# Two pairs' places 960 to 1008 sorted in one pass, and the next pair's first rows gathered beside a node sort

## The chip, the cores and the metric

The kernel runs on one core of one Trainium2 chip. The metric is device time in microseconds (us) for one execution. Before the change the median of three executions was 3306.28 us (3271.85 to 3311.16).

## What is computed

There are 16 graphs of 1024 nodes, each node with 64 channels. Layer 0 is the part that the change touches. It normalises and clips the nodes, drops some edges of nodes with many neighbours, and then takes for every node and channel three quantiles over the node's remaining neighbours:

```python
vals = jnp.where(nd[..., None], x[:, None, :, :], jnp.inf)
s = jnp.sort(vals, axis=2)
nv = nd.sum(2)
for tau, w in zip((0.25, 0.5, 0.75), (0.25, 0.5, 0.25)):
    pos = tau * jnp.maximum(nv - 1, 0)
    lo, hi = jnp.floor(pos), jnp.ceil(pos)
    agg = agg + w * (v_lo + (pos - lo) * (v_hi - v_lo))
```

The sum goes through two small matmuls and is added to x. Layer 1 is three graph convolutions with the whole adjacency and a last matmul.

## The kernel before

**Places.** The graphs are handled as 8 pairs, p = 0 to 7, with the two graphs of a pair in the upper and lower 64 partitions. The nodes of a graph are ordered by their number of neighbours, and a node's position in that order is its place. Places with similar counts share a sorting network with a fixed number of slots. Places 0 to 640 are three *blocks* (0: 200 places with 11 slots, 1: 192 with 13, 2: 248 with 15), places 640 to 960 are three groups of *nodes* (17, 19 and 21 slots), 960 to 1008 are one more block, called MID here (48 places, 26 slots), and 1008 to 1024 are the TAIL (16 places, 42 slots).

**How rows get to their slots.** For a block, `gather` (L1115) makes one-hot matrices `s` on VectorE (L1143) for two or more slots at a time, and TensorE multiplies them with the node values `hp` into PSUM (L1174); ScalarE copies the result to the tile `g` (L1179). The values are in three bfloat16 parts, `st.hp`, and no such matmul can run before the third part is written (L698). There are two buffers for `s`. For nodes, GpSimd issues one indirect DMA for each slot and graph (`ask`, L1287), 34, 38 or 42 for a sort; here they are called asks. Their target `gn` is one buffer, so a new set of asks starts when the sort before it has read its rows.

**How rows are sorted.** `quantiles` (L1070) runs a network of min and max on VectorE (L1081), each instruction over several slots at once, multiplies the ranks that are wanted with coefficients (L1093) and adds them up (L1102). An instruction's width is the number of compared slots times the places. TAIL is sorted for four pairs at once: a pair's TAIL rows go to DRAM (`tail_d`, L1230), and `rows_of_pairs` (L1251) loads them beside each other. MID is sorted for each pair alone.

**The order.** For each of the pairs 0 to 6 the loop runs these stages one after the other; `weave` (L1335) puts steps of other work between the instructions of a sort, at set shares of it:

1. sort block 0, with the gather of block 1 and asks;
2. sort nodes, with the gather of block 2;
3. sort block 1, with asks for the next nodes;
4. sort block 2, with the gathers of MID and TAIL and asks;
5. sort nodes, with the last 9 steps (`steps(4)`) of `prepare` for pair p+1;
6. after pair 4 only: sort the TAIL of pairs 0 to 3;
7. sort MID of pair p, with the gather of block 0 of pair p+1 and 0.4 of the asks for the next nodes.

Through all of it the steps of `prepare(p + 1)` (L637) are spread: loading the adjacency, dropping edges, listing the rows, numbering the slots, writing `hp`. Pair 7 has the same stages after the loop, with `later` woven in instead: the two dense layers of all pairs. `later` begins by fetching the sums of a pair with 16 indirect DMAs (L1474), and VectorE adds them up (L1371).

The order in the source is not the order on the engines: a planner in the framework estimates when each instruction is ready and sorts each engine's stream by it. Every engine then runs its own stream strictly in order, so that an instruction which waits holds up all that stand behind it on its engine.

**Tags.** Tiles with one tag share a buffer: `g0` holds the rows of blocks 0 and 2 and the TAIL rows of several pairs, `g1` those of block 1 and MID.

Of the kernel before, what the change touches and what calls it, by code (L numbers as in the profile page):

```python
# [406 lines left out]
def graph_layers_kernel(ctx: ExitStack, tc: tile.TileContext, ins, out: bass.AP):  # L407
# [187 lines left out]
    def layernorm_relu(pool, h, xt, sq, T):  # L595
# [17 lines left out]
    live_d = [dram.tile([N, N // 4], I32, name=f"live_d{b}") for b in range(NB)]  # L613
    MW, TW = (b[1] - b[0] for b in (BLOCKS[MID], TAIL))
    part_d = {
        MID + 1: [dram.tile([P, TAIL[3], TW], F32, name=f"tail_d{p}") for p in range(NP)],
    }

    with tc.tile_pool(name="setup_fill", bufs=1) as setup:
# [5 lines left out]
                nc.scalar.dma_start(out=rows_d[p][x * ROWS + ZERO_ROW : x * ROWS + BIG_ROW + 1, :], in_=filler)  # L625

    part_z = {
        MID: const.tile([P, len(TAUS), 1, MW], BF16, name="mid_z"),
        MID + 1: const.tile([P, len(TAUS), NP, TW], BF16, name="tail_z"),
    }  # L630
    place = const.tile([P, NB, NT], I32, name="place")
# [478 lines left out]
    def per_group(block):  # L1110

        W = block[1] - block[0]
        return max(1, min(HALF // W, 400 // W))
# [98 lines left out]
    def gather_block(st, n, pools, home=None, into=None, first=-0.2, end=0.9):  # L1212


        work, ps, rows = pools
        block = (BLOCKS + (TAIL,))[n]
        j0, j1, _, slots = block
        pool, tag, bufs = home or (rows, f"g{n % 2}", 1)

        def groups():  # L1220
            if n >= MID:
                z = part_z[n]
                nc.scalar.copy(z[:, :, st.p % z.shape[2], :], st.z[:, :, slice(*held(block))])
            to = into
            if to is None:
                to = st.g[n] = pool.tile([P, slots, j1 - j0], F32, tag=tag, bufs=bufs, name="g")
            send(pools, (yield from gather(st, block, to, pools)))
            in_place = n == MID or st.p == NP - 1
            if n >= MID and not in_place:
                nc.scalar.dma_start(out=part_d[n][st.p][:, :, :], in_=to)  # L1230

        return Steps(groups()), -(-slots // per_group(block)), first, end

    def sort_block(st, n, pools):

        work, ps, rows = pools
        block = BLOCKS[n]
        j0, j1, _, slots = block
        if n == 0:

            send(pools, st.gathered)
            st.agg = work.tile([P, SPLIT], F32, tag="agg", bufs=1, name="agg")
            st.done = 0
        t = rows.tile([P, plan(block)[3], j1 - j0], F32, tag="t", bufs=1, name="t")
        yield from quantiles(work, block, (st.g[n], t), st.z[:, :, j0:j1], st.agg[:, j0:j1])
        while st.done + P <= j1:
            cols = slice(st.done, st.done + P)
            waiting.append((st.p, st.agg, cols, st.done))
            st.done = cols.stop

    def rows_of_pairs(n, first, end, sent, pools, tag):  # L1251

        work, ps, rows = pools
        block = (BLOCKS + (TAIL,))[n]
        W = block[1] - block[0]
        g = rows.tile([P, block[3], (end - first) * W], F32, tag=tag, bufs=1, name="g_pairs")
        for p in range(first, sent):
            nc.scalar.dma_start(out=g[:, :, (p - first) * W : (p - first + 1) * W], in_=part_d[n][p][:, :, :])
        return g
# [42 lines left out]
    def asking(fetched, first, end, share=1.0):  # L1302

        return fetched[4], math.ceil(share * NODES[fetched[1]][3]), first, end
# [346 lines left out]
    with ExitStack() as stack:  # L1651
        keep = stack.enter_context(tc.tile_pool(name="keep", bufs=1))
        pools = (
            stack.enter_context(tc.tile_pool(name="work", bufs=1)),
            stack.enter_context(tc.tile_pool(name="ps", bufs=1, space=PSUM)),
            stack.enter_context(tc.tile_pool(name="rows", bufs=1)),
        )
        with ExitStack() as inner:
            early = (
                inner.enter_context(tc.tile_pool(name="early", bufs=1)), keep,  # L1660
                inner.enter_context(tc.tile_pool(name="ps_early", bufs=1, space=PSUM)),
            )
            ahead = Steps(prepare(0, early))
            ahead.rest()
            sts = [ahead.result]
            jobs = iter(NODE_ORDER)

            def fetch_next(tag="gn"):
                pairs, i = next(jobs)
                return fetch_nodes([sts[p] for p in pairs], i, pools, tag)  # L1670

            nodes = fetch_next()
            nodes[4].rest()
            first, *_ = gather_block(sts[0], 0, pools)
            first.rest()
            for p in range(NP - 1):
                st = sts[p]
                ahead = Steps(prepare(p + 1, early))

                def steps(n):  # L1680
                    return ahead, SHARES[n], 0.0, 1.0

                weave(sort_block(st, 0, pools), gather_block(st, 1, pools), asking(nodes, 0.0, 0.9), steps(0))
                weave(sort_nodes(nodes, pools), gather_block(st, 2, pools), steps(1))
                nodes = fetch_next()
                weave(sort_block(st, 1, pools), asking(nodes, 0.1, 1.0, 0.4), steps(2))
                send_nodes()
                both = rows_of_pairs(MID, p, p + 1, p, pools, "g1")
                weave(
                    sort_block(st, 2, pools), gather_block(st, MID, pools, into=both),  # L1690
                    gather_block(st, MID + 1, pools, (early[0], "a", 2)), asking(nodes, 0.0, 0.7), steps(3),
                )
                if p in TAILS:
                    tails = rows_of_pairs(MID + 1, *TAILS[p], TAILS[p][1], pools, "g0")
                weave(sort_nodes(nodes, pools), steps(4))
                ahead.rest()
                sts.append(ahead.result)
                nodes = fetch_next()
                if p in TAILS:
                    weave(sort_pairs(MID + 1, *TAILS[p], tails, pools))  # L1700
                    send(pools)
                weave(
                    sort_pairs(MID, p, p + 1, both, pools), gather_block(sts[-1], 0, pools, first=0.3, end=1.0),
                    asking(nodes, 0.0, 1.0, 0.4),
                )


        with ExitStack() as inner:
            one = inner.enter_context(tc.tile_pool(name="late", bufs=1))
            late = (one, inner.enter_context(tc.tile_pool(name="ps_late", bufs=2, space=PSUM)))  # L1710
            done = Pair()
            done.sent = 4
            ahead = Steps(later(late, keep, done))
            def steps(n):
                return ahead, LATE_SHARES[n], 0.0, 1.0

            st = sts[-1]
            weave(sort_block(st, 0, pools), gather_block(st, 1, pools), asking(nodes, 0.0, 0.9), steps(0))
            weave(sort_nodes(nodes, pools), gather_block(st, 2, pools), steps(1))
            nodes = fetch_next()  # L1720
            then = [fetch_next("r0")]
            weave(sort_block(st, 1, pools), asking(nodes, 0.0, 0.9), steps(2))
            send_nodes()
            both = rows_of_pairs(MID, NP - 1, NP, NP - 1, pools, "g1")
            weave(
                sort_block(st, 2, pools), gather_block(st, MID, pools, into=both), asking(then[0], 0.0, 0.9), steps(3)
            )
            tails = rows_of_pairs(MID + 1, *TAILS[NP - 1], NP - 1, pools, "g0")
            weave(sort_nodes(nodes, pools), gather_block(st, MID + 1, pools, into=tails[:, :, -TW:]), steps(4))
            then += [fetch_next(), fetch_next("s"), fetch_next("s")]  # L1730
            weave(
                sort_pairs(MID + 1, *TAILS[NP - 1], tails, pools), asking(then[1], 0.0, 0.5), asking(then[2], 0.5, 1.0),
                steps(5),
            )
            send(pools)
            done.sent = NP - 2
            weave(sort_nodes(then[0], pools), asking(then[3], 0.0, 1.0), steps(6))
            send_nodes()
            weave(sort_pairs(MID, NP - 1, NP, both, pools), steps(7))
            send(pools)  # L1740
            weave(sort_nodes(then[1], pools), steps(8))
            send_nodes()
            done.sent = NP - 1
            weave(sort_nodes(then[2], pools), steps(9))
            send_nodes()
            weave(sort_nodes(then[3], pools), steps(10))
            send(pools)
            done.sent = NP
            ahead.rest()
# [46 lines left out]
```

## Time and profile before

| | us |
|---|---|
| median of three executions | 3306.28 |
| the profiled execution | 3037.03 |
| its span, first to last instruction | 3035.3 |
| VectorE busy (L1081 is its largest line) | 2410.4 |
| TensorE busy, mean granted clock 0.861 | 2116.4 |
| GpSimd busy, most of it L1287 | 1551.3 |
| the 744 asks L1287 | 1182.9 |
| pair 0: nodes (second), MID, then block 0 of pair 1 | 42.8 + 39.2 + 43.2 |
| pair 4: nodes, TAIL, MID, then block 0 of pair 5 | 44.4 + 60.8 + 33.0 + 46.4 |
| pair 6: nodes, MID, then block 0 of pair 7 | 49.4 + 91.0 + 39.1 |
| last MID sort, of pair 7 | 55.8 |

The profiled execution took 269 us less than the median. The rows by stage run from one sort's last addition on VectorE to the next one's. Loop and preparation take the first 2208 us; the rest is pair 7 and the dense layers.

### The profile page before, as it was taken

How to read it: one execution, taken by the hardware profiler on the slowest of the kernel's cores; microseconds unless marked ns; L12 is line 12 of the kernel's file. 1: busy time of each engine (PE TensorE's matmuls, PEld its weight loads, DVE VectorE, ACT ScalarE, POOL GpSimd, SP SyncE). 2: the span in 40 equal slices, each digit the busy share in tenths (PEclk: the TensorE clock that was granted, in tenths of full speed). 3: DMA queues.
4: the chain of work that ended last, by engine and by line, in shares of the span. 5: the costliest groups of instructions: out<-in, count | busy, mean ns of one | idle time of the engine just before them, and what ended most of it. 6: DMA issues, size and time to landing. Idle time of an engine off the chain costs nothing. (4 is left out here: it accounts for less than half of the span.)

```text
span 3035.3 us, 58595 instructions
## 1 busy us (share of the span) xinstructions
PE 2116.4 (70%) x23385; PEld 1480.7 (49%) x23401; DVE 2410.4 (79%) x5602; ACT 1563.8 (52%) x3060; POOL 1551.3 (51%) x1155
## 2 busy tenths in 40 slices
PE   1748876886887688678627886886368487067768
PEld 0435744663565466356414753663256264034446
DVE  3238989999998999999899999998378489268732
ACT  2775775676487468557634775687023123022212
POOL 5115556385645738564675285374834768730110
PEclk9879988997998899799858997997689698588889
DMA  4214123322321332232312221412211242112211
GB/s 120 73 45 124 56 68 73 102 65 62 99 91 46 75 99 62 62 109 86 65 36 67 88 63 51 135 56 52 67 19 21 64 85 69 25 21 53 56 50 44
DMA packets 261051, 205.54 MB, mean 68 GB/s; under 512 B 217120, under 2 KB 217248, under 8 KB 256672
## 3 DMA queue, kind: packets, MB, share of 16 engines
q1 hardware_dynamic: 165120, 131.39, 15.1%
q0 software_dynamic: 39680, 62.23, 8.3%
q10 hardware_dynamic: 55968, 8.09, 1.6%
q8 instruction: 185, 3.03, 0.4%
q14 instruction: 98, 0.80, 0.1%
HBM read 148.82 MB, written 52.75 MB: 66 GB/s over the span
## 5 line engine op out<-in xcount | busy, mean ns | idle before, releaser
L1287 POOL DMA_INDIRECT g_nodes<-rows_d,rows_listed x744 | 1182.9, 1590 | 907.0 <-DVE prod L1093 310.5
L1174 PE MATMUL pg<-s,hp 128*64 128x248 bf16 (+6 forms) x12048 | 888.1, 301 | 171.7 <-DVE s L1143 150.2
L1174 PEld LDWEIGHTS <-hp 128*64 128x64 bf16 x12048 | 656.8, 114 | 349.3 <-DVE s L1143 101.5
L1143 DVE TENSOR_SCALAR s<-r 128x3200 bf16<-128x3200 bf16 (+19 forms) x856 | 406.1, 523 | 36.0 <-PE pg L1174 34.8
L1429 PE MATMUL pg<-adjT,xw 128*64 128x512 fp8e4 x2304 | 282.3, 399 | 60.2 <-ACT xw L1418 56.3
L1474 POOL DMA_INDIRECT agg<-agg_d,place x128 | 131.4, 1027 | 275.3 <-DVE rest L1417 138.5
L890 POOL DMA_INDIRECT live_d<-edge,place x128 | 170.7, 1334 | 146.5 <-DVE place L883 108.4
L1429 PEld LDWEIGHTS <-xw 128*64 128x64 bf16 x2304 | 149.2, 115 | 177.4 <-ACT xw L1418 64.2
L787 PE MATMUL ptE<-ident_h,edge 128*128 128x128 bf16 x1024 | 86.1, 236 | 212.6 <-ACT edge L780 191.7
L1179 ACT COPY g<-pg 128x248 f32<-128x248 f32 (+3 forms) x238 | 97.7, 411 | 247.3 <-PE pg L1174 246.7
L1371 DVE TENSOR_TENSOR agg<-agg,h_late 128x1024 f32<-128x1024 f32 x8 | 9.8, 1230 | 243.1 <-DMA agg<-agg_d,place 243.1
L780 ACT ACTIVATE edge<-a 128x1024 fp8e4<-128x1024 f32 x128 | 134.7, 1054 | 95.5 <-DMA a<-in_adj 79.3
L787 PEld LDWEIGHTS <-edge 128*128 128x128 fp8e4 x1024 | 66.4, 105 | 236.6 <-ACT edge L780 199.8
L782 DVE SCALAR_TENSOR_TENSOR junk_v<-a 128x1024 fp8e4<-128x1024 f32 x128 | 155.8, 1217 | 27.7 <-DMA a<-in_adj 27.0
L1081 DVE TENSOR_TENSOR t<-g 128x800 f32<-128x800 f32 (+9 forms) x184 | 167.5, 924 | 0.9
L880 ACT ACTIVATE stays<-keys,minus 128x1024 fp8e4<-128x1024 f32 x128 | 143.3, 1119 | 37.5 <-PE keys L872 32.7
L1081 DVE TENSOR_TENSOR g<-t 128x992 f32<-128x992 f32 (+7 forms) x176 | 160.0, 932 | 1.8
L924 PE MATMUL pt<-ident_h,lp 128*128 128x128 bf16 x1024 | 94.3, 250 | 89.5 <-DMA lp<-live_d 43.2
L834 ACT ACTIVATE stays<-cs,back 128x1024 f16<-128x1024 f32 x128 | 137.1, 1113 | 34.2 <-DVE look L815 16.0
L861 ACT ACTIVATE edge<-q,bias 128x1024 fp8e4<-128x1024 f32 x128 | 141.8, 1109 | 17.4 <-PE q L856 16.7
L1081 DVE TENSOR_TENSOR t_nodes<-g_nodes 128x256 f32<-128x256 f32 (+6 forms) x192 | 125.2, 659 | 31.8 <-DMA g_nodes<-rows_d,rows_listed 19.2
L790 ACT ACTIVATE edgeT<-ptE 128x1024 fp8e4<-128x1024 f32 x128 | 129.8, 1038 | 17.3 <-PE ptE L787 16.5
(241 smaller groups left out, 4530.8 us busy)
## 6 DMA issues: line engine op xcount, KB each, us to landing
a<-in_adj SPq DMA_DIRECT2D x128, 512.0 KB
adjT_d<-edgeT SPq DMA_DIRECT2D x16, 1024.0 KB
lp<-live_d POOLq DMA_DIRECT2D x32, 512.0 KB
adjT<-adjT_d SPq DMA_DIRECT2D x16, 1024.0 KB
g_nodes<-rows_d,rows_listed POOLq DMA_INDIRECT x744
room<-in_x SPq DMA_DIRECT2D x16, 256.0 KB
h_d<-room SPq DMA_DIRECT2D x16, 256.0 KB
rows_d<-room SPq DMA_DIRECT2D x64, 64.0 KB
```

Of the source, the lines that this page charges most:

```text
L780: nc.scalar.activation(edge[:, t, :], a, AF.Sign, saturate=False)
L782: nc.vector.scalar_tensor_tensor(junk, a, 1.0, a, ALU.is_equal, ALU.not_equal, accum_out=odd[:, b, t : t + 1], saturate=False)
L787: nc.tensor.matmul(out=pt[:, u, :], lhsT=edge[:, t, u * P : (u + 1) * P], rhs=ident_h, start=True, stop=True)
L834: nc.scalar.activation(stays[:, t, :], cs, AF.Abs, bias=back[:, t : t + 1], scale=2.0)
L861: nc.scalar.activation(edge[:, t, :], q, AF.Relu, bias=bias(-2.0), accum_out=nv[:, t : t + 1], saturate=False)
L880: nc.scalar.activation(junk, keys, AF.Sign, bias=minus[:, t : t + 1], accum_out=above[:, t : t + 1], saturate=False)
L890: sent = nc.gpsimd.indirect_dma_start(out=live_d[b][:, :], out_offset=bass.IndirectOffsetOnAxis(ap=place[:, b, t : t + 1], axis=0), in_=ed ...
L1081: nc.vector.tensor_tensor(view(bufs, o, n1, n2), view(bufs, a, n1, n2), view(bufs, b, n1, n2), ALU.max if op else ALU.min)
L1143: nc.vector.tensor_scalar(s[:, k, :, us, w0:], r[:, :, us, at + w0 : at + W], float(LIVE + 1 + k0 + k), None, ALU.is_equal)
L1174: summed = nc.tensor.matmul(out=pg[x * C : (x + 1) * C, ks, w0:], lhsT=st.hp[:, part, x, u, :], rhs=s[:, ks, x, u, w0:], start=(whole and ...
L1287: nc.gpsimd.indirect_dma_start(out=g[:, k, a * C : (a + 1) * C], out_offset=None, in_=rows_d[st.p][:, :], in_offset=bass.IndirectOffsetOnA ...
L1429: nc.tensor.matmul(out=pg[cs, :], lhsT=part[:, u, cs], rhs=adjT[x][:, u, sl], start=(u == 0 and k == 0), stop=(u == NT - 1 and k == len(xw ...
```

## The change

MID is no longer sorted after every pair, but after every odd one for that pair and the even one before it: four sorts of 96 places, where there were eight of 48. An even pair's MID rows are written to DRAM (`mid_d`) on ScalarE's queue and loaded again beside the odd pair's in stage 4 of the odd pair. With no MID sort in an even pair, the gather of block 0 of the next pair is woven with the node sort of stage 5, from half of it on, behind the last steps of `prepare`, which are squeezed into the first 0.4 of it; in pair 4 it goes with the TAIL sort. The asks that stood beside MID are given in the next stage 1 alone. The rows of several pairs' TAIL in the loop move from `g0` to `g1`. Pair 7's MID sort holds pairs 6 and 7.

```diff
@@ -613,6 +613,7 @@
     part_d = {
+        MID: [None if p % 2 else dram.tile([P, BLOCKS[MID][3], MW], F32, name=f"mid_d{p}") for p in range(NP)],
         MID + 1: [dram.tile([P, TAIL[3], TW], F32, name=f"tail_d{p}") for p in range(NP)],
     }
@@ -625,7 +626,7 @@
-        MID: const.tile([P, len(TAUS), 1, MW], BF16, name="mid_z"),
+        MID: const.tile([P, len(TAUS), 2, MW], BF16, name="mid_z"),
@@ -1225,7 +1226,7 @@
-            in_place = n == MID or st.p == NP - 1
+            in_place = (n == MID and st.p % 2) or st.p == NP - 1
             if n >= MID and not in_place:
                 nc.scalar.dma_start(out=part_d[n][st.p][:, :, :], in_=to)
@@ -1685,24 +1686,45 @@
-                both = rows_of_pairs(MID, p, p + 1, p, pools, "g1")
+                both = rows_of_pairs(MID, p - 1, p + 1, p, pools, "g1") if p % 2 else None
                 weave(
-                    sort_block(st, 2, pools), gather_block(st, MID, pools, into=both),
+                    sort_block(st, 2, pools), gather_block(st, MID, pools, into=both and both[:, :, MW:]),
                     gather_block(st, MID + 1, pools, (early[0], "a", 2)), asking(nodes, 0.0, 0.7), steps(3),
                 )
                 if p in TAILS:
-                    tails = rows_of_pairs(MID + 1, *TAILS[p], TAILS[p][1], pools, "g0")
-                weave(sort_nodes(nodes, pools), steps(4))
-                ahead.rest()
-                sts.append(ahead.result)
-                nodes = fetch_next()
-                if p in TAILS:
-                    weave(sort_pairs(MID + 1, *TAILS[p], tails, pools))
+                    tails = rows_of_pairs(MID + 1, *TAILS[p], TAILS[p][1], pools, "g1")
+
+                def coming():
+                    ahead.rest()
+                    sts.append(ahead.result)
+                    steps, *_ = gather_block(sts[-1], 0, pools)
+                    yield from steps.gen
+
+                coming = Steps(coming())
+                count = -(-BLOCKS[0][3] // per_group(BLOCKS[0]))
+                if p % 2:
+                    weave(sort_nodes(nodes, pools), steps(4))
+                    ahead.rest()
+                    coming_at = 0.3
+                elif p in TAILS:
+                    weave(sort_nodes(nodes, pools), steps(4))
+                    ahead.rest()
+                    weave(sort_pairs(MID + 1, *TAILS[p], tails, pools), (coming, count, 0.4, 1.0))
+                    coming.rest()
                     send(pools)
-                weave(
-                    sort_pairs(MID, p, p + 1, both, pools), gather_block(sts[-1], 0, pools, first=0.3, end=1.0),
-                    asking(nodes, 0.0, 1.0, 0.4),
-                )
+                else:
+                    weave(sort_nodes(nodes, pools), (ahead, SHARES[4], 0.0, 0.4), (coming, count, 0.5, 1.0))
+                    coming.rest()
+                if p % 2:
+                    coming.step()
+                    nodes = fetch_next()
+                    weave(
+                        sort_pairs(MID, p - 1, p + 1, both, pools), (coming, count, 0.3, 1.0),
+                        asking(nodes, 0.0, 1.0, 0.4),
+                    )
+                    coming.rest()
+                else:
+                    nodes = fetch_next()
@@ -1721,9 +1743,9 @@
-            both = rows_of_pairs(MID, NP - 1, NP, NP - 1, pools, "g1")
+            both = rows_of_pairs(MID, NP - 2, NP, NP - 1, pools, "g1")
             weave(
-                sort_block(st, 2, pools), gather_block(st, MID, pools, into=both), asking(then[0], 0.0, 0.9), steps(3)
+                sort_block(st, 2, pools), gather_block(st, MID, pools, into=both[:, :, MW:]), asking(then[0], 0.0, 0.9), steps(3)
             )
@@ -1736,7 +1758,7 @@
-            weave(sort_pairs(MID, NP - 1, NP, both, pools), steps(7))
+            weave(sort_pairs(MID, NP - 2, NP, both, pools), steps(7))
```

## The prediction

> **What bounds the kernel now.** I read the busy shares first, then the 40 slices, then the windows of single stages, then who waited for whom. The chain that ended last covers only the final layers and says nothing of the loop.
>
> ```profile
> PE 2116.4 (70%) x23385; PEld 1480.7 (49%) x23401; DVE 2410.4 (79%) x5602; ACT 1563.8 (52%) x3060; POOL 1551.3 (51%) x1155
> DVE  3238989999998999999899999998378489268732
> ```
>
> VectorE (DVE) is at 90% or more in the slices of the loop (260 to 2130 us), so there its instructions set the time. The next fence is the windows of pair 1: second node sort, MID, block 0 of pair 2. Columns are length, then busy us and instructions of each engine, granted clock, DMA share, GB/s.
>
> ```profile
> core 0: us, PE busy (x) PEld busy (x) DVE busy (x) ACT busy (x) POOL busy (x), PEclk, DMA share, GB/s
> 685.00:729.50 44.50, 30.76 (x264) 16.37 (x265) 41.08 (x136) 33.38 (x69) 14.02 (x13) 0.79 0.19 59
> 729.50:769.00 39.50, 26.47 (x313) 17.18 (x313) 39.16 (x120) 15.79 (x37) 35.67 (x13) 0.80 0.21 54
> 769.00:819.00 50.00, 38.74 (x456) 27.17 (x457) 44.75 (x61) 27.48 (x52) 37.25 (x25) 0.90 0.52 148
> ```
>
> MID fills VectorE (39.2 of 39.5 us) and covers 26.5 us of TensorE: the gather of the next block 0. In a timeline inside such a stage, the start of one sort instruction to the next is what it costs, less than its duration:
>
> ```profile
> 2142.32 0.35 DVE L1081 TENSOR_TENSOR t_pairs<-t_pairs 128x192 f32<-128x192 f32 x1
> 2142.59 0.25 DVE L1081 TENSOR_TENSOR t_pairs<-g_pairs 128x96 f32<-128x96 f32 x1
> 2142.76 0.35 DVE L1081 TENSOR_TENSOR t_pairs<-g_pairs,t_pairs 128x192 f32<-128x192 f32 x1
> ...
> 2148.07 0.20 DVE L1081 TENSOR_TENSOR t_pairs<-g_pairs,t_pairs 128x48 f32<-128x48 f32 x1
> 2148.19 0.38 DVE L1081 TENSOR_TENSOR g_pairs<-t_pairs,g_pairs 128x48 f32<-128x48 f32 x2
> ```
>
> Widths 192, 96 and 48 start the next after 0.27, 0.17 and 0.12 us: 1.04 ns a column and 69 ns fixed. The 0.20 to 0.35 us durations overlap, and summing them would promise twice the saving.
>
> Two waits matter: GpSimd's asks inside MID, and VectorE's wait at the end of MID of pair 6.
>
> ```profile
> 735.01 1.14 POOL L1287 DMA_INDIRECT g_nodes<-rows_d,rows_listed  x1 [0.30 <-issue]
> 736.45 11.96 POOL L1287 DMA_INDIRECT g_nodes<-rows_d,rows_listed  x1 [0.30 <-issue]
> 748.71 0.94 POOL L1287 DMA_INDIRECT g_nodes<-rows_d,rows_listed  x1 [0.30 <-issue]
> ```
>
> ```profile
> 2201.18 0.94 POOL L1474 DMA_INDIRECT agg<-agg_d,place  x1 [0.30 <-issue]
> ...
> 2203.67 1.27 DVE L1371 TENSOR_TENSOR agg<-agg,h_late 128x1024 f32<-128x1024 f32 x1 [52.22 <-DMA agg<-agg_d,place]
> ```
>
> **What the Trainium skill says.** *Vector Engine (DVE) Microarchitecture Reference*, section 5.2, gives 1.0417 ns a column and about 75 ns an instruction after overlap; the starts above agree (1.04 and 69). *SBUF — State Buffer*, section "Who interferes with whom", says that GpSimd and VectorE share a port pair that one instruction holds whole, and that a tensor_tensor with both inputs in SBUF contends with GpSimd's reads. The trace fits: an ask takes 0.94 us while VectorE is idle (2152 to 2182 us), 1.3 to 1.7 us in block 0, and two of them 10 to 15 us in a MID sort. *TensorE: Matmul & The Clock Gate*, section "What's actually happening", has the clock throttled by default and released by activity; granted clocks in my windows run from 0.60 to 0.98, low where TensorE is idle. It serves the slow rival.
>
> **The change part by part.**
>
> *Four MID sorts fewer.* A MID sort is 91 instructions (89 in pair 4) and 12,768 columns: 91 x 0.069 + 12,768 x 0.00104 = 19.6 us. Even pairs lose it: -19.6 in pairs 0 and 2, -18.9 in pair 4. An odd pair's sort keeps its 91 instructions and doubles the columns: +13.3 us each in pairs 1, 3, 5 and 7. Were nothing but VectorE in play, that is 4 x (19.6 - 13.3) = -25 us. ScalarE's stream loses 55 rows, mostly coefficients; at 52% busy I value that at nothing (cover: VectorE's sorts; without that cover, a gain under 1 us for each of four sorts).
>
> *Pairs 0 and 2: the gather loses its cover.* In the built order only four of block 0's one-hot instructions (two groups, all that two `s` buffers hold) stand inside the node sort. The third group stands behind the last write of `hp`, which stands at or after the end of the node sort. TensorE's part of this gather took 25.3 us in pair 0 (484.4 to 509.7, from 2 us after `hp`). Block 0's sort needs slots 0 to 6 first (four of six groups) and then the rest. Between `hp` and the instruction that needs the last slots, pair 0's order has seven one-hot instructions of this gather (5.7 us), four adjacency checks L782 (5.2), four one-hots of block 1 (3.3) and two 600-wide sort instructions (1.4): 15.6 us beside 25.3 + 2, so VectorE idles some 11 us, where MID hid it all. Bounds: 7 (clock 0.98 instead of 0.91) to 20 (clock 0.65). Net -8.6 in each of pairs 0 and 2.
>
> *The asks.* From the point where `gn` and its list are free to the next node sort's first instruction VectorE has some 70 us of work in these pairs, idle time included. The 34 and 38 asks at 1.7 us (block 0's pace, with gaps) need 58 and 65, plus some 2 to land. They fit, barely: 0, with 0 to +10 each. What would be late next is that node sort.
>
> *Pair 4.* The gather goes beside 60.8 us of TAIL sort, in which TensorE was busy 2.1 us. Fully covered: -18.9. The asks of that stage have TAIL and block 0, 107 us; 0. The TAIL rows in `g1` must wait for the write of `mid_d`, and ScalarE waits with them: 0 to +7, as the longest issue of such a load took 7.1 us; I take 0, because the node sort follows.
>
> *Odd pairs 1, 3, 5.* +13.3 each. The asks get that much longer, so the waits before the next node sort (5.2 us at 817, 3.5 at 1348) shrink; I take -5 in all. Sum +35.
>
> *The DRAM trip.* Writes are long rows. A load has 128 x 26 pieces of 192 bytes. ScalarE's DMA queue took 1.6% of 16 engines x 3035 us for 55,968 packets, 14 ns each, so 3328 on 16 engines are 3 us, issued a whole block 2 ahead of the sort. Its issue waits for block 1's rows in `g1`, with ScalarE's evacuations behind it: 0 to +7 for each of four; I take 0, the cover being VectorE's block 2.
>
> *Pair 6 and the dense layers.* Before, 38 asks from 2109.6 took until 2182 (two were held 11 us each by MID), then came 16 fetches of sums, and L1371 ran at 2203.7, 94 us after the start. L1371 now stands after the fourth group of the block 0 gather, and GpSimd's order has all 42 asks ahead of the fetches. VectorE reaches it 30 us after the start; 18 asks at 1.6 us, 24 at the free pace of 1.25, 16 fetches at 1.25 and the landing make 81 us. So the stall stays, about 50 us. The last two groups and the `s` buffers behind it cost 6 us more than before. Net 81 + 6 - 94 = -7, not the -19.6 of its sort. Bounds -20 and +10.
>
> *Pair 7's MID.* +13.3, but a wait of 14.4 us for L1371 (2740.7) stands in that stage, and the sort work ahead of it that runs beside the fetches costs nothing: +5, bounds 0 and 13.
>
> Sum: -17.2 - 18.9 + 35 - 7 + 5 = **-3 us** against the profiled 3037. The median of the runs is 269 us higher and the profile does not show where; I carry the difference over unscaled: 3306 - 3 = **3303 us**. This case's own range is 3268 to 3348, from the bounds above.
>
> **The rivals.**
>
> *Slower, the gather without cover (21%).* After `hp`, TensorE has block 0's 25 us, block 1's (4.6 us for each of seven groups, 32) and the next adjacency's transposes (about 10): 67 us beside some 63 of VectorE work up to the next node sort. At the clock seen there, 0.91, it just fits. If the long idle phases drop it below 0.75, the 67 become over 81 and each of pairs 0, 2 and 6 loses another 18 us or more; at 0.65, 94 and 31, so +93 - 3: 3396. For it: clocks of 0.69 and 0.65 in the windows of pair 2's node sort and pair 6's MID, and the runs' extra 269 us, which may be TensorE's. Against: in these stretches TensorE is busy almost throughout.
>
> *Faster, the stall of pair 6 goes too (15%).* If L1371's 52 us no longer block and the even gathers stay covered, it is -25 - 52 = -77: 3229. Against it stands the built order, with 58 GpSimd instructions ahead of that wait.
>
> *Nothing moves.* If the 269 us are TensorE's and it is the bound in the timed runs, both saving and cost vanish: 3306, inside the likeliest case.
>
> **Chances.** A measurement of this kernel can tell about 2% (66 us) from no change. Within it: 64%, forecast and null together. Faster by more: 15%; slower by more: 21%. The range for 8 in 10 reaches into both rivals: 3230 to 3390.
>
> **What would show it.** Right: MID sorts of 96 places near 33 us of starts; in pairs 0 and 2 idle time of 7 to 20 us on L1143 or on the first L1081 of block 0, released by TensorE; no asks of 10 us there; a 45 to 55 us wait of the first L1371. Wrong: idle over 25 us in those pairs, node sorts that wait for asks, a ScalarE held by the `mid_d` loads, or an L1371 that finds its rows.

## The result and the profile after

The changed kernel takes 3403.55 us (median of four, 3399.71 to 3406.83), the kernel before 3291.27 in the same comparison: ratio 1.034, 95% interval 1.026 to 1.042. It is 3.4% slower; forecast were 3303 us and no change. A later comparison on another chip gave 1.042 (1.031 to 1.053). All ratios here leave out executions more than 1.5% above the fastest of their kernel, so that they can differ a little from the quotient of the medians.

The page of the changed kernel, the lines that answer to those shown of before: busy time of each engine, and VectorE in the 40 slices.

```profile
PE 2235.3 (66%) x23401; PEld 1493.6 (44%) x23401; DVE 2391.6 (70%) x5238; ACT 1552.4 (46%) x2988; POOL 1331.7 (39%) x1155
DVE  4136885979879598599799975997176381388852
```

VectorE has 19 us less work than before, and yet it is at 90% or more in 11 of the 40 slices where it was in 21: it waits. The next fence is the windows of the changed kernel at three hand-overs from one pair to the next: block 0 after the node sort in pairs 0 and 2, and the sort of 96 places in pair 3. Columns are length, then busy us and instructions of each engine, TensorE's granted clock, DMA share, GB/s.

```profile
core 0: us, PE busy (x) PEld busy (x) DVE busy (x) ACT busy (x) POOL busy (x), PEclk, DMA share, GB/s
532.60:635.60 103.00, 71.78 (x740) 41.40 (x741) 62.38 (x87) 41.61 (x77) 35.04 (x34) 0.76 0.36 100
1137.50:1232.40 94.90, 64.47 (x744) 41.34 (x742) 53.43 (x80) 36.44 (x71) 37.12 (x36) 0.82 0.33 94
1406.40:1500.30 93.90, 34.82 (x374) 22.22 (x374) 57.87 (x158) 24.07 (x64) 29.22 (x31) 0.66 0.17 36
```

In each of them VectorE is idle for 36 to 41 us (length less busy time). Two waits in the first two windows make most of it, from the timeline of VectorE ("remote" is an end that the profile can put down to no instruction):

```profile
583.23 1.90 DVE L1144 TENSOR_SCALAR s<-r 128x3200 bf16<-128x3200 bf16 x2 [26.36 <-remote]
1189.61 3.37 DVE L1144 TENSOR_SCALAR s<-r 128x2688 bf16<-128x2688 bf16 x4 [31.79 <-remote]
```

A one-hot that waits for its `s` buffer waits for TensorE. But in such stretches the trace shows "issue" as what TensorE waited for, which means nothing that the profile knows: its inputs were there.

**The shown trace of before is not like its other executions.** It took 3037 us where they took about 3290, so the two traces can't be subtracted. A second trace of the kernel before, unchanged (`b_again`, 3361 us), has what the first lacks. TensorE in the first gather of block 0, in the second trace:

```profile
244.13 0.33 PE L1174 MATMUL pg<-s,hp 128*64 128x400 bf16 x1
245.43 0.33 PE L1174 MATMUL pg<-s,hp 128*64 128x400 bf16 x1 [0.97 <-issue]
246.14 0.36 PE L1174 MATMUL pg<-s,hp 128*64 128x400 bf16 x2 [0.38 <-issue]
246.85 0.33 PE L1174 MATMUL pg<-s,hp 128*64 128x400 bf16 x1 [0.35 <-issue]
248.27 0.36 PE L1174 MATMUL pg<-s,hp 128*64 128x400 bf16 x2 [1.09 <-issue]
```

and the same gather in the trace shown with the prediction:

```profile
244.75 2.03 PE L1174 MATMUL pg<-s,hp 128*64 128x400 bf16 x22
246.61 0.25 PE L1168 MATMUL pg<-none,ident_big 128*64 128x200 bf16 x2
246.69 3.72 PE L1174 MATMUL pg<-s,hp 128*64 128x400 bf16 x42
```

One or two matmuls start every 0.7 us or a multiple of it, where 22 should start in 2.03 us. Below such a stretch is called a choke. I count a run of at least eight waits for "issue" of over 0.25 us from start to start, with a median of 0.6 to 1.5 us. By this count the chokes are 0 us in the first trace of before, 369 in the second and 393 in the changed kernel's. A count depends on where a stretch is taken to end, by some tens of us for the large ones, and those under 30 us can come out as nothing.

### The profile page after: what moved, and what is told of

The parts are those of the page before. It is cut to its first block, busy times and chain, and to the rows that moved or that the text cites. A ratio compares the mean times of both kernels' runs of the same rounds, so it can differ in the third digit from the quotient of the medians.

```text
span 3400.8 us, 58161 instructions
## 1 busy us (share of the span) xinstructions
PE 2235.3 (66%) x23401; PEld 1493.6 (44%) x23401; DVE 2391.6 (70%) x5238; ACT 1552.4 (46%) x2988; POOL 1331.7 (39%) x1155
## 3 DMA queue, kind: packets, MB, share of 16 engines
q1 hardware_dynamic: 165120, 131.39, 13.3%
q0 software_dynamic: 39680, 62.23, 7.3%
## 5 line engine op out<-in xcount | busy, mean ns | idle before, releaser
L1288 POOL DMA_INDIRECT g_nodes<-rows_d,rows_listed x744 | 966.0, 1298 | 1194.2 <-DVE prod L1094 555.8
L1175 PE MATMUL pg<-s,hp 128*64 128x248 bf16 (+6 forms) x12048 | 957.1, 304 | 390.1 <-issue 142.2
L1430 PE MATMUL pg<-adjT,xw 128*64 128x512 fp8e4 x2304 | 308.3, 402 | 157.9 <-issue 144.3
L1180 ACT COPY g<-pg 128x248 f32<-128x248 f32 (+4 forms) x254 | 103.9, 411 | 416.6 <-PE pg L1175 204.9
L891 POOL DMA_INDIRECT live_d<-edge,place x128 | 165.7, 1294 | 286.2 <-DVE place L884 250.2
L783 DVE SCALAR_TENSOR_TENSOR junk_v<-a 128x1024 fp8e4<-128x1024 f32 x128 | 155.8, 1218 | 28.1 <-DMA a<-in_adj 28.0
L1434 ACT ACTIVATE xT<-pg,c_L_gnn_b 128x512 f32<-128x512 f32 x48 | 32.9, 685 | 272.9 <-PE pg L1430 137.6
L862 ACT ACTIVATE edge<-q,bias 128x1024 fp8e4<-128x1024 f32 x128 | 141.8, 1109 | 28.1 <-PE q L857 25.4
L1435 DVE TENSOR_SCALAR xT<-xT,bn_s,c_L_gnn_be 128x512 f32<-128x512 f32 x48 | 26.1, 543 | 175.0 <-ACT xT L1434 175.0
L826 PE MATMUL cs<-before,sums 128*128 128x512 bf16 x256 | 109.3, 427 | 51.0 <-ACT stays L835 25.2
```

The source lines that it names most:

```text
L783: nc.vector.scalar_tensor_tensor(junk, a, 1.0, a, ALU.is_equal, ALU.not_equal, accum_out=odd[:, b, t : t + 1], saturate=False)
L862: nc.scalar.activation(edge[:, t, :], q, AF.Relu, bias=bias(-2.0), accum_out=nv[:, t : t + 1], saturate=False)
L891: sent = nc.gpsimd.indirect_dma_start(out=live_d[b][:, :], out_offset=bass.IndirectOffsetOnAxis(ap=place[:, b, t : t + 1], axis=0), in_=ed ...
L1175: summed = nc.tensor.matmul(out=pg[x * C : (x + 1) * C, ks, w0:], lhsT=st.hp[:, part, x, u, :], rhs=s[:, ks, x, u, w0:], start=(whole and ...
L1288: nc.gpsimd.indirect_dma_start(out=g[:, k, a * C : (a + 1) * C], out_offset=None, in_=rows_d[st.p][:, :], in_offset=bass.IndirectOffsetOnA ...
L1430: nc.tensor.matmul(out=pg[cs, :], lhsT=part[:, u, cs], rhs=adjT[x][:, u, sl], start=(u == 0 and k == 0), stop=(u == NT - 1 and k == len(xw ...
```

## The experiments

Every choke counted in both kernels lies in a run of GpSimd's indirect DMAs: mostly asks (L1287, in the changed kernel L1288), in the dense layers fetches of sums as well, in some places a few writes of `prepare` (L890, L891). When nothing holds GpSimd, asks start every 1.25 us; the choke sets in while they do, and most end 2 to 10 us after the last one. Hence the theory "asks choke TensorE", against the supply of instructions, the current that the array draws, and the prediction's slow rival.

Chokes are those of the traced execution (for `b_zero` and `b_move` one of 3357 and one of 3414 us), the free pace is from ask to ask where nothing holds them, both in us. Memset times are those where nothing holds GpSimd (the expectations give means over all of them, 0.56 and 0.34).

| run | what differs | us | ratio to before | free pace | chokes |
|---|---|---|---|---|---|
| `b_again` | before, unchanged | 3361 | single | 1.25 | 369 |
| `a_again` | changed, unchanged | 3479 | 1.042 | 1.25 | 374 |
| `b_zero`, `a_zero` | gathered values zero | 3339, 3447 | 0.995, 1.025 | 1.25 | 416, 336 |
| `b_move` | only the gather moved | 3391 | 1.009 | 1.25 | 486 |
| `b_plain`, `a_plain` | plain DMAs for asks | 2844, 2865 | 0.850, 0.856 | none | 15, 40 |
| `b_paced8`, `a_paced8` | memset of 0.10 us | 3291, 3467 | 0.988, 1.038 | 1.26 | 254, 373 |
| `b_paced256`, `a_paced256` | memset of 0.30 us | 3117, 3160 | 0.935, 0.949 | 1.41 | 26, 55 |
| `b_paced`, `a_paced` | memset of 0.51 us | 3170, 3154 | 0.947, 0.942 | 1.62 | 27, 43 |
| `a_paced2x` | two such memsets | 3501 | 1.053 | 2.20 | 51 |
| `a_even`, `a_odd` | 0.51 us, some sets | 3393, 3368 | 1.023, 1.015 | mixed | 193, 349 |
| `a_hand`, `b_hand` | 0.51 us, six sets | 3332, 3380 | 0.998, 1.013 | mixed | 265, 361 |

A ratio's 95% interval is ±0.003 to 0.014. The kernel before took 3329 to 3347 (median) in these comparisons, and single executions 3291 to 3377. The chokes of the two unchanged kernels are alike (369 and 374), so the loss is not that there is more of it: it depends on where it falls.

**Is the choke old, and is it the data?**

> The kernel before, unchanged, for a second trace. Its shown trace took 3037 us while its other executions took about 3290; the trace of the changed kernel (3403 us) has TensorE stretches of 20 to 50 us in which matmuls start only every 0.70 or 1.40 us with nothing to wait for, and the shown trace of before has none. Theory 'choked TensorE': the kernel before has such stretches too in an ordinary execution, about 250 us of them in all, and takes about 3290. Rival 'the change brings them': no such stretch, and the extra 250 us lie elsewhere, spread over all engines or at the start.

It is old: 14 stretches in the kernel before, more in all than the 250 us expected.

```diff
         st.hp = keep.tile([P, 3, 2, NT, C], BF16, tag="hp", name="hp")
+        nc.scalar.mul(h, h, 0.0)
         nc.scalar.copy(st.hp[:, 0], h)
```

> The kernel before with the gathered values set to zero on ScalarE before they are split (one more ScalarE instruction of about 1.5 us for each pair): the sorts see zeros, the aggregates of the blocks are left out; every matmul, its size and its order stay. If the choke depends on the current that the array draws ('choked by the data'), it goes from the gathers (L1174), and the kernel takes 3040 to 3150. If it is the supply of instructions or anything that data do not touch, nothing changes: 3270 to 3320.

> The changed kernel with the same zeros. 'Choked by the data': the stretches of spaced matmuls go from the gathers, and it stands within 30 us of the kernel before with zeros, 3040 to 3150. 'Supply of instructions': 3390 to 3410 as without. 'Lost cover and clock' (the slow rival of the prediction, in which the gather is slow because TensorE is idle before it): also unchanged, as the idle time before it stays.

Zeros take 0.5% off the kernel before (0.992 to 0.998), where 6% or more were to go, and the distance between the two kernels stays at 108 us. What the gathered values draw is not it.

**One part of the change alone.** The gather is woven beside the node sort in pairs 0, 2 and 6, and each pair still sorts its own MID:

```diff
+                if p % 2 == 0 and p not in TAILS:
+                    coming = Steps(coming())
+                    count = -(-BLOCKS[0][3] // per_group(BLOCKS[0]))
+                    weave(sort_nodes(nodes, pools), (ahead, SHARES[4], 0.0, 0.4), (coming, count, 0.5, 1.0))
+                    coming.rest()
+                    nodes = fetch_next()
+                    weave(sort_pairs(MID, p, p + 1, both, pools), asking(nodes, 0.0, 1.0, 0.4))
+                    continue
```

> The kernel before, with one part of the change: in pairs 0, 2 and 6 the gather of the next block 0 is woven beside the node sort as in the changed kernel, but every pair still sorts its own places 960 to 1008 right after it, beside the asks. If the loss of the change comes from the gather that has no VectorE work of its own beside it, the sort of 20 us behind it still covers most of it: within 25 us of the kernel before. If the loss comes from TensorE doing this gather in one dense burst wherever it stands, about two thirds of the change's 110 us show here: 3350 to 3390.

Ratio 1.009 (1.005 to 1.012), some 28 us (the medians lie 45 apart): between the two theories, and about a quarter of the change's loss. It doesn't decide between them; the place of the gather alone is not the whole cause.

**Asks taken away.** Six plain DMAs on GpSimd's queue bring the same bytes for each node sort, in fewer and larger packets (24,064 on that queue for 39,680); which row goes to which node is left out:

```diff
-                    nc.gpsimd.indirect_dma_start(
...
+                    if k % 8 == 0:
+                        n = min(8, slots - k)
+                        nc.gpsimd.dma_start(
+                            out=g[:, k : k + n, a * C : (a + 1) * C],
+                            in_=rows_d[st.p][: n * P, :].rearrange("(t p) c -> p t c", p=P),
+                        )
```

> The kernel before with GpSimd's indirect asks (L1287, 34 to 42 in a run) replaced by four to six plain DMAs on the same queue that bring as many bytes in rows of 256 bytes; which rows belong to which node is left out. In all traces of both kernels the stretches of spaced matmuls lie within long runs of asks that follow each other every 1.25 us, and end 2 to 10 us after the last ask of the run. Theory 'asks choke TensorE': without asks the stretches are gone (under 30 us in all, where the second trace of before has about 330), and the kernel takes 2950 to 3080. Rival 'supply of instructions runs dry by itself' (pages of 16 KB for every 256 TensorE instructions): the stretches stay, above 200 us, and the time stays over 3250.

> The changed kernel with the same plain DMAs in place of the asks. 'Asks choke TensorE': no such stretches, 2930 to 3080, and beside the kernel before with plain DMAs it shows what the change is worth without the choke: the sum of the prediction, -3, without its terms for asks about -20, give or take 30. 'Supply runs dry': over 3350. 'Lost cover and clock': still 60 us or more above the kernel before with plain DMAs.

Both get 14 to 15% faster, more than expected (without asks the node sorts don't wait for them either), and the chokes are nearly gone; the one of `b_plain` lies beside 12 fetches of sums, indirect DMAs that stayed, at 1.25 us. The page of `b_plain`, busy times and VectorE's slices:

```profile
PE 2088.2 (74%) x23385; PEld 1455.0 (51%) x23401; DVE 2404.3 (85%) x5602; ACT 1562.0 (55%) x3060; POOL 492.9 (17%) x531
DVE  3217999999999999999999999999977898878822
```

TensorE has its 23,385 matmuls as before, and VectorE its nines again. This also rules out the rival of the supply. The Trainium skill, *Runtime: NRT & Kernel Launch*, section "Instruction fetch mechanics", has the sequencer fetch blocks of 16 KiB, 256 instructions, ahead of their use. The traces agree (185 packets of 16,384 bytes on the instruction queue, about 255 TensorE records between two), but the supply is the same in `b_plain`, and the choke is not there.

**What of the change is left without asks.** The same three hand-overs in the windows of `a_plain`:

```profile
472.20:547.00 74.80, 58.92 (x740) 38.70 (x741) 62.53 (x87) 41.44 (x77) 0.00 (x0) 0.89 0.42 123
1009.40:1073.50 64.10, 56.72 (x744) 39.94 (x742) 53.31 (x80) 36.38 (x71) 0.00 (x0) 0.99 0.44 133
1238.10:1298.40 60.30, 33.55 (x374) 21.44 (x373) 57.33 (x157) 23.16 (x63) 0.00 (x0) 0.78 0.15 39
```

The same work of VectorE (62.5, 53.3 and 57.3 us) in 28, 31 and 34 us less. What is left of idle time in the first window is the gather without cover; VectorE's waits there:

```profile
490.77 1.89 DVE L1144 TENSOR_SCALAR s<-r 128x3200 bf16<-128x3200 bf16 x2 [5.88 <-PE pg L1175]
494.58 1.89 DVE L1144 TENSOR_SCALAR s<-r 128x3200 bf16<-128x3200 bf16 x2 [1.91 <-PE pg L1175]
498.73 1.73 DVE L1144 TENSOR_SCALAR s<-r 128x3072 bf16<-128x3072 bf16 x2 [2.25 <-PE pg L1175]
```

They sum to 10.0 us; all idle time of the window is 12.3, of the second 10.8.

**Asks spaced.** A memset on GpSimd after each ask, held in place by scheduling dependences that cost no semaphore:

```diff
+                    behind(asked)
+                    behind(nc.gpsimd.memset(pace, 0.0))
```

> The kernel before, with a GpSimd memset of about 0.5 us after each ask, so that the asks of a free run come every 1.8 us and not every 1.25. 'Asks choke TensorE' by their rate: fewer and shorter stretches, and a gain of 100 to 250 us, less what the longer runs of asks hold up the node sorts (up to 60). If it is the presence of asks at any rate, the stretches get longer with the runs: 3350 to 3500. 'Supply runs dry': no shorter stretches, 3300 to 3420.

> The changed kernel with the same memsets. By the rate: a gain of 150 to 350 us on 3403, with pairs 0, 2 and 6 losing no more than 30 us each to their gathers. At any rate: 3420 to 3600. Beside the kernel before with memsets it shows whether the change costs anything but the choke.

> All asks spaced as in the run with memsets of 0.56 us (1.8 us from ask to ask at the free pace, ratio 0.942), but with memsets half as long: about 1.55 us. A threshold in the rate between 1.25 and 1.55 us gives 0.93 to 0.95, or better, as the node sorts wait less for their asks; a choke in proportion to the rate gives about 0.98 to 1.0.

> The kernel before with all asks spaced by a memset of 0.34 us, as in the run of the changed kernel that stood at 0.949. The sum of the prediction (-3 us, -20 without its terms for waits on asks) then says 0.949 to 0.957 here; what plain DMAs showed (the change costs 21 us) says 0.941 to 0.944.

> Two such memsets of 0.56 us after each ask: 2.4 us from ask to ask. What is left of the choke at 1.8 us (four stretches, 43 us) goes; but 38 asks then need 90 us, more than the 70 that a pair has for them, so every node sort waits 15 to 30 us: slower than at 1.8 us, 0.97 to 1.05. If the choke at 1.8 us was still large and hidden, it gets faster: under 0.93.

> The kernel before with a memset of 8 elements (about 0.1 us) after each ask. If the pace is what slows TensorE, asks still come every 1.2 to 1.25 us and nothing changes: ratio 0.98 to 1.02. If it is asks back to back, the stretches go and the node sorts wait less than with longer memsets: 0.91 to 0.94.

> The changed kernel with the same. If the pace decides: 1.02 to 1.05, as without memsets. If back to back decides: 0.91 to 0.95, and the difference to the kernel before with the same memsets is what the change itself is worth: -0.5% by the run with 0.56 us, +0.7% by the plain DMAs.

It is the pace. At 1.26 us from ask to ask the choke stays, although a memset stands between (so back to back is not the condition); at 1.41 it is nearly gone. The limit lies between these two. At 2.2 us the expected waits of the node sorts come (315 us for their rows, 61 in `a_paced`), and cost more than the choke. TensorE and GpSimd side by side in the first gather of `b_paced256`, where the choke of `b_again` began (44 matmuls without a break, at a granted clock of 0.63):

```profile
239.82 6.15 PE L1185 MATMUL pg<-s,hp 128*64 128x400 bf16 x44
240.35 0.30 POOL L1305 MEMSET pace<- 1x256 bf16 x1
240.82 0.95 POOL L1298 DMA_INDIRECT g_nodes<-rows_d,rows_listed  x1 [0.16 <-issue]
241.76 0.30 POOL L1305 MEMSET pace<- 1x256 bf16 x1
242.23 0.95 POOL L1298 DMA_INDIRECT g_nodes<-rows_d,rows_listed  x1 [0.16 <-issue]
```

`b_paced256`, the kernel before with one memset more for each ask, is the fastest version with all of the computation: 3117 us, 6.5% under the kernel before (0.926 to 0.944), a little below both expectations. It doesn't hold the change.

**Where the change meets it.** The memsets only at some hand-overs: after those of pairs 0, 2 and 6 (`a_even`), of 1, 3 and 5 (`a_odd`), of all six (`a_hand`, `b_hand`).

> The changed kernel with the memset of 0.56 us after each ask only for the sets of asks that are given at the end of pairs 0, 2 and 6, beside the gather that the change moved. If the change's loss of 3.4% lies in these gathers ('asks choke the uncovered gather'), the three stages (nodes, then block 0) lose 20 to 30 us each and the whole about 75: ratio to before 1.00 to 1.02. If the asks beside the sorts of 96 places in pairs 1, 3 and 5 carry it, nothing is gained here: 1.03 or more. The prediction's slow rival, a gather slowed by TensorE's clock, also says 1.03 or more.

> The changed kernel with the memsets only for the asks given at the end of pairs 1, 3 and 5, beside the sort of 96 places. There the trace shows 34 and 38 us in pairs 3 and 5 beyond the same stages with plain DMAs, while a ScalarE copy of the numbering waits 6 us and more for TensorE. 'Asks choke TensorE' wherever VectorE does not hold them: these two stages lose 30 us each, ratio to before 1.01 to 1.02. If only the moved gather matters: 1.03 or more.

> The changed kernel with the memset of 0.56 us after each ask of the six sets given at the end of pairs 0, 1, 2, 3, 5 and 6, and of no others. If the loss lies in these hand-overs, this and the kernel before with the same six sets spaced stand within 1% of each other, both at 0.98 to 1.00. If the choke comes back in other stages in equal amount, it stays 2% or more above that one.

> The kernel before with the same six sets spaced. Its hand-overs hold some 80 us of choke (pairs 0, 2 and 6 above all), so 0.98 to 1.00; if its sorts of 48 places already hold the asks long enough, nothing is gained: 1.00 to 1.01.

`a_again` beside the last two:

> The changed kernel, unchanged, beside the others on one chip: ratio to before 1.03, as at first (1.026 to 1.042). Under 1.02 would say that the loss differs from chip to chip as much as the effects measured here.

Measured against `a_plain`, the hand-overs of pairs 0, 2 and 6 stood 27, 28 and 35 us above it in the changed kernel and 3, 3 and 15 in `a_even`; those of pairs 3 and 5 stood 31 and 38 above it, and 0 and 7 in `a_odd`. `a_even` gained less in all than expected, because the first node sorts and blocks 1 and 2 of pairs 1 and 2 took 53 us more than in the changed kernel's first trace; `a_again` has the same 53 us there without a memset, so this varies between executions. With all six sets spaced the changed kernel falls from 1.042 to 0.998, the kernel before doesn't gain (1.013, above both of its expectations). The loss lies in these hand-overs: they make 120 of the 131 us between the traces of `a_again` and `b_again`.

But not in all of them alike. `b_again` stands above `b_plain` as well, by 24, 5 and 40 us in pairs 0, 2 and 6, and by 2 and 0 in pairs 3 and 5. So pairs 0 and 6 lost as much before the change; it adds some 27 us in pair 2 and 40 each in pairs 3 and 5.

**Why there.** In the kernel before a MID sort holds the asks. The window of MID of pair 3 in `b_again` (columns as above), and GpSimd in it:

```profile
1416.80:1455.40 38.60, 25.64 (x313) 18.04 (x313) 38.60 (x117) 16.96 (x46) 37.10 (x5) 0.83 0.18 48
```

```profile
1415.31 1.44 POOL L1287 DMA_INDIRECT g_nodes<-rows_d,rows_listed  x1 [32.68 <-DVE single L712]
1417.06 31.81 POOL L1287 DMA_INDIRECT g_nodes<-rows_d,rows_listed  x1 [0.31 <-issue]
1449.18 2.09 POOL L1287 DMA_INDIRECT g_nodes<-rows_d,rows_listed  x1 [0.30 <-issue]
```

While one ask is held for 31.8 us, TensorE gathers undisturbed. In the changed kernel even pairs have no such sort there, and in odd pairs one step of the gather is taken before the sort (`coming.step()`), so that a one-hot stands behind its first instruction. VectorE, ScalarE, and the last four of the matmuls on TensorE, in the same stage of the changed kernel:

```profile
1438.80 1.03 DVE L1144 TENSOR_SCALAR s<-r 128x3200 bf16<-128x3200 bf16 x1 [30.44 <-ACT r L983]
```

```profile
1419.88 0.69 ACT L983 CAST r<-pr 128x640 bf16<-128x640 f32 x1 [5.96 <-remote]
1427.58 0.69 ACT L983 CAST r<-pr 128x640 bf16<-128x640 f32 x1 [7.01 <-remote]
1438.08 0.69 ACT L983 CAST r<-pr 128x640 bf16<-128x640 f32 x1 [9.53 <-remote]
```

```profile
1420.63 0.59 PE L977 MATMUL pr<-liveT,upto 128*128 128x512 fp8e4 x1 [5.81 <-ACT r L983]
1421.01 0.63 PE L979 MATMUL pr<-sums,before 128*128 128x512 bf16 x1
1421.43 0.31 PE L977 MATMUL pr<-liveT,upto 128*128 128x128 fp8e4 x1
1421.54 0.31 PE L979 MATMUL pr<-sums,before 128*128 128x128 bf16 x1
```

The one-hot waits for the last copy of the numbering, and each copy for four short matmuls. By the count above this is no choke: the four run one after the other, as soon as a buffer is free. What is late is the copy. These four end at 1421.85, and the copy of them is the one at 1438.08, 16 us later; for the three sets before it is 6, 11 and 13 us (the ends of matmuls are modelled). In `a_plain` the last three copies start 0.04 to 0.15 us after their matmuls, and the same one-hot waits 1.63 us:

```profile
1241.64 0.99 DVE L1144 TENSOR_SCALAR s<-r 128x3200 bf16<-128x3200 bf16 x1 [1.63 <-ACT r L983]
```

VectorE, waiting, no longer holds the asks, and they run free at 0.94 us each. With these asks spaced the last two copies start within 0.2 us of their matmuls and the loss of the stage is gone (`a_odd`), so it is they that make the copies late. That a wait of VectorE thus feeds itself through GpSimd is how I read the two traces; what starts it was not tried apart.

## Why the prediction was wrong

Terms of its sum, in us, beside the hand-overs (second node sort, TAIL, MID and the block 0 after it) of the runs:

| step | forecast | `a_plain` less `b_plain` | `a_again` less `b_again` |
|---|---|---|---|
| pair 0, gather without cover | -8.6 | -5.8 | -0.9 |
| pair 2, the same | -8.6 | -3.9 | +23.4 |
| pair 4, covered by TAIL | -18.9 | -26.9 | -28.1 |
| pairs 1, 3, 5 | +13.3 each, -5 in all | +14.3, +22.3, +17.5 | +11.0, +63.4, +56.5 |
| pair 6 | -7 | +0.4 | -5.8 |
| MID of pair 7 | +5 | +11.3 | not used |

- **Four MID sorts fewer:** right. From the start of each sort instruction to the next one's on VectorE, a sort of 48 places takes 19.6 us (forecast 19.6), one of 96 takes 32.8 (33): 13.2 more, forecast 13.3.
- **Pairs 0 and 2, idle time of 11 us (7 to 20):** right without asks, 12.3 and 10.8. In the changed kernel it was 41 and 41.
- **The asks, "They fit, barely: 0":** this step failed. It priced an ask by GpSimd's time alone. They fitted, at 1.25 us each and not at 1.7, as VectorE was idle, and at that pace they choke TensorE: beside the gathers of pairs 0 and 2 VectorE idled 41 us and not 11. The sign that I named as right, no ask of 10 us there, came true and was the harm: the asks of 10 us and more in the MID sorts were what kept the pace down. The shared port of GpSimd and VectorE that the prediction cites was read as a cost only.
- **Odd pairs, +13.3 each and asks that wait 5 us less:** failed with it, and this is the largest part: +35 forecast, +131 measured (+54 without asks). Pairs 3 and 5 cost 40 us each beyond what they cost with plain DMAs. The sum has no term for a one-hot behind the first instruction of MID that waits 30 us for TensorE and ScalarE.
- **Pair 4:** fully covered, as said, and 8 us better. Its asks ran beside TAIL, which holds them.
- **DRAM trip and ScalarE held: 0:** right. The loads from `mid_d` took 0.54 to 0.60 us to issue, and one wait of 0.6 us stood behind them. MID of pair 7, +11 without asks, is inside its bounds of 0 and 13.
- **Pair 6:** the size was right by luck. The first L1372 (L1371 before) was to wait 45 to 55 us and found its rows without a wait, a sign that the prediction named as wrong. VectorE came late to it: the one-hots ahead of it had waited 45.5 and 12.9 us for the gather.
- **The 269 us:** "I carry the difference over unscaled" treated them as a constant. They go with the chokes, 369 us of them in `b_again` and none in the shown trace, and a change that moves asks and gathers changes what these cost. That they "are TensorE's" was among the rivals, but as a case in which nothing moves.

The slow rival, 3396, is near the measured 3404 by luck. It had the gathers without cover slowed by TensorE's clock. The clock was lower there (0.76 and 0.82, with plain DMAs 0.89 and 0.99), but it followed: with the asks gone the same two windows hold 59 and 57 us of TensorE and not 72 and 64, and with the asks spaced (`a_hand`) the first holds 59 at a clock of 0.87. And some 80 us of the loss lie in pairs 3 and 5, where it had none. (The clocks that the prediction read, 0.60 to 0.98, went down to 0.50 in pair 4's TAIL.)

Without chokes the change is worth little: -0.5% with memsets of 0.51 us (3154 against 3170), +0.7% with plain DMAs (2865 against 2844), +1.5% with 0.30 us, between two comparisons on two chips (0.949 against 0.935). The forecast's -3 us is inside that.

## What to carry to other kernels

A trace that is much faster than the median is a trace of another regime: take a second one before anything is subtracted or costed. An engine that waits for "issue" in evenly spaced bursts is to be set beside what all other engines do in just these stretches, since an instruction may cost an engine that it doesn't work with, as the asks did here. A conflict that slows one party can protect a third, so ask what runs free once it is gone.

## What the runs showed of the hardware

Long runs of GpSimd's indirect DMAs at one every 1.25 us bring TensorE down to one or two matmuls in 0.7 to 1.4 us, with operands ready; at one every 1.41 us they hardly do (26 and 55 us of choke for 369 and 374). ScalarE's copies behind TensorE can then start 6 to 16 us after their matmuls, while TensorE's matmuls start 0.06 us after ScalarE. The values gathered don't matter (0.5%), nor do the bytes moved (plain DMAs with as many don't do it). What the two share was not found. The Trainium skill, *DMA: Bandwidth & Descriptors*, section "SWDGE vs HWDGE vs iDMA", says that GpSimd computes the descriptors of its DMAs in software and writes them to rings in SBUF; that this is the path was not tried. Nor is it known why one execution of the kernel before went without a choke: its asks ran at the free pace too, but for no more than 11 in a row while TensorE had work. Whether shorter runs do no harm, or runs are only short where no choke lets VectorE wait, these traces can't tell.
